# Attention with conditioned heads: the kept exponentials of every fourth step in place of second scores

## The chip, the cores and the metric

The kernel runs on one core of one Trainium2 chip. The metric is the device time of one execution in microseconds (us). One execution of the kernel before was also recorded by the hardware profiler; the page, the busy times by stretch, the chain of waits and the timelines of the engines that are shown below all come from that one execution.

## The reference

Eight batches of 512 rows with 512 features go through one attention layer with 16 heads of 32 features, and the result is added to the input. The conditioning vector of a batch is projected by the same weights and added to the queries and the keys.

```python
Q = split_heads(x @ Wq.T + bq);  K = split_heads(x @ Wk.T + bk);  V = split_heads(x @ Wv.T + bv)
cQ = Q + split_heads(tokens @ Wq.T + bq)
cK = K + split_heads(tokens @ Wk.T + bk)
scores = einsum('bhqd,bhkd->bhqk', cQ, cK) / sqrt(32)
attn = softmax(scores, axis=-1)
out = einsum('bhqk,bhkd->bhqd', attn, V)
return x + merge_heads(out)          # x: (8, 512, 512), all float32
```

## The kernel before

**Steps.** The work is cut into T = 32 steps. Step t is batch t // 4 and a group of four heads (t % 4); the four heads lie in the four groups of 32 partitions. The scores of a step are computed twice. The *row scores* (`row_scores`, L526) have a query row in each partition, 128 query rows at a time (`qc`, four of them): VectorE takes each row's maximum (`one_max` L494, `row_max_of` L535), and ACT takes the exponentials of the row with the maximum as bias (`denominators`, L545), of which only their sum is used: the 512 exponentials go to a tile named "dead". The *second scores* (`exponentials`) have a key in each partition, 128 keys at a time (`kc`): a matmul of ones with the transposed maxima `maxT` subtracts the maximum (L597), the product of keys and queries is accumulated on it (L600), and ACT writes the exponentials to tiles "e" (L611). These have the layout that the product with the values needs (`times_v`, L616).

**The maxima** reach `maxT` in this way: POOL splits each into three bf16 parts (`split_max`, L559 to L562), and a transposing DMA on SP's queue turns them (`turn_max`, L571). The second scores of the next step begin with it.

**The loop** runs over t from 0 to T - 4 (L833). A step has four items. Each does the second scores of step t for one `kc`, the row scores of step t + 1 (the last item: of step t + 2) for one `qc`, and then one more piece of work on TensorE:

- first item: part of the projection q of the next batch; second item: the values of step t - 1 (`weighted`, L616; this item is called V below); third item: part of k; fourth: part of v.
- A projection is done for two head groups at a time by a scheme of seven block products (`product`, L407): `first_products` in one step (VectorE: a copy m1 at L442, then adds at L451, L452, L429 or L432), `other_products` in the following one (adds at L465, L466, L429 or L432). The sums of input blocks that the scheme needs, `xc`, are made by `combine_x` on VectorE.
- VectorE also turns the input blocks (`turn_x`, L323) and the results (`send`, L672) in 32x32 blocks; POOL scales the result and adds the residual (L673, L674), which `load_residual` has loaded and to which POOL has added a bias (L173).

The last three steps (T - 3 to T - 1) have code of their own.

**Order.** The order on PE, ACT, VectorE and POOL is the order in which the program writes the instructions. SP issues nearly all the DMAs from one queue, in an order that the framework's scheduler sets; a DMA there that waits holds up those behind it.

**PSUM.** All eight banks are one ring tile. Which bank plays which part (four for the second scores, four for the row scores, two of these again for the item's own product) is a written table, `TURNS`, of one row per item.

Of the kernel before, what the change touches and what calls it, by code (L numbers as in the profile page):

```python
# [9 lines left out]
F32 = mybir.dt.float32  # L10
BF16 = mybir.dt.bfloat16
# [6 lines left out]
def kernel(  # L18
# [51 lines left out]

    const = ctx.enter_context(tc.tile_pool(name="const", bufs=1))
    stage = ctx.enter_context(tc.tile_pool(name="stage", bufs=3))
    xp = ctx.enter_context(tc.tile_pool(name="xp", bufs=4))
    xtp = ctx.enter_context(tc.tile_pool(name="xtp", bufs=2))
    qkp = ctx.enter_context(tc.tile_pool(name="qkp", bufs=3))
    ep = ctx.enter_context(tc.tile_pool(name="ep", bufs=13))
# [33 lines left out]
    turn = [0]  # L110

    def banks(i, n=1):

        j = TURNS[turn[0]][i]
        if n == 1:
            return psum[:, j, :]
        k = TURNS[turn[0]][i + 1]
        return psum[:, j : k + 1 : k - j, :]

    def advance():  # L120
        turn[0] = {7: 0, len(TURNS) - 1: 4}.get(turn[0], turn[0] + 1)
# [10 lines left out]
    def load_x(n, queue=nc.sync):  # L132

        if n < B * NS:
            xs[n] = xp.tile([P, D], F32, tag="x", name=f"x_{n}")
            queue.dma_start(xs[n], x[n // NS, n % NS * P : (n % NS + 1) * P, :])
# [16 lines left out]
    xr = {}  # L153

# [4 lines left out]
    def load_residual(t):  # L159

        b, g = divmod(t, G)
        if turned_by_vector(t):
            xr[t] = op.tile([P, NB, BL], F32, tag="xr", name=f"xr_{t}", bufs=3)
            for h in range(HG):
                nc.sync.dma_start(
                    xr[t][h * BL : (h + 1) * BL], spread(x[b], g * P + h * BL)
                )
            bias = bvs[:, g, :].unsqueeze(1).broadcast_to([P, NB, BL])
        else:

            xr[t] = xT[b][:, g, :]
            bias = bvl.broadcast_to([P, S])
        nc.gpsimd.tensor_tensor(xr[t], xr[t], bias, ALU.add)  # L173

    ws = {}
# [23 lines left out]
    wk0 = op.tile([P, D], F32, tag="dead", name="wk0")  # L199
    nc.scalar.dma_start(wk0, Wk[:P, :])  # L200

    cond_sb = const.tile([B + 2, D], F32, tag="cond", name="cond_sb")
# [33 lines left out]
    split = []  # L236
    for i in range(2):
        m = const.tile([P, NS, HG, HD], BF16, tag=f"split{i}", name=f"split{i}")
        nc.vector.memset(m, 0.0)
        split.append(m)  # L240
# [62 lines left out]
    def transpose_x(n, pt, leaves=nc.vector.tensor_copy):  # L303

        b, sc = divmod(n, NS)
        if b >= B:
            return
        if sc == 0:
            xT[b] = xtp.tile([P, NC, S], F32, tag="xT", name=f"xT_{b}")
        for cc in range(NC):  # L310
            nc.tensor.transpose(  # L311
                pt[:, cc * P : (cc + 1) * P], xs[n][:, cc * P : (cc + 1) * P], ident
            )
        leaves(xT[b][:, :, sc * P : (sc + 1) * P], pt.rearrange("p (c s) -> p c s", c=NC))
        load_block(n + NC)

    def turn_x(n):
        b, cc = divmod(n, NC)
        if b >= B:
            return  # L320
        if cc == 0:
            xT[b] = xtp.tile([P, NC, S], F32, tag="xT", name=f"xT_{b}")
        nc.vector.transpose(xT[b][:, cc, :], xs[n].rearrange("p f i -> p (f i)"))  # L323
        load_block(n + NC)
# [129 lines left out]

    def other_products(n, b, u, dens, small, at):

        dens()
        one_, two_ = banks(at[0]), banks(at[1])
        product(n, b, u, 4, one_[:, :HS])
        product(n, b, u, 5, one_[:, HS:])  # L460
        small()
        product(n, b, u, 2, two_[:, :HS], (1,))
        product(n, b, u, 3, two_[:, HS:])
        c1, c12, c2, c22 = parts_of(n, b, u)
        nc.vector.tensor_tensor(c12, one_[:, HS:], c12, ALU.add)  # L465
        nc.vector.tensor_tensor(c2, halves(one_), twice(c22), ALU.add)  # L466
        plus(n, b, u, 0, c1, halves(two_), c1)
        if n != "v":
            for g in range(2):
                qkT[n, b * G + u * 2 + g] = pair_of(b * G + u * 2, n)[:, g, :]  # L470
# [27 lines left out]
    def row_max(t, qc, hold=False):  # L498

        if t >= T:  # L500
            return
        open_max(t)
        for j in range(HG):
            row_scores(t, qc, j, banks(HG + j))
        if t < T - 2 or t * NS + qc == T * NS - 1:
            for j in range(2):
                one_max(t, qc, j, banks(HG + j))
        else:
            row_max_of(t, qc, 0, banks(HG, 2))
        last, both = [banks(HG + 2), banks(HG + 3)], banks(HG + 2, 2)  # L510

        def held():
            if hold and t < T - 2:
                for j in range(2):
                    one_max(t, qc, 2 + j, last[j])
            else:
                row_max_of(t, qc, 1, both)

        if hold:
            return held  # L520
        held()
        return nothing
# [16 lines left out]
    def denominators(t, qc, prs=range(NP)):  # L539

        if t >= T - 2:
            return
        for j in [pr * 2 + i for pr in prs for i in range(2)]:
            dead = op.tile([P, S], F32, tag="dead", name=f"dead_{t}_{qc}_{j}")
            nc.scalar.activation(  # L545
                dead,
                banks(HG + j),
                AF.Exp,
                bias=nmax[t][:, qc, j, :],
                accum_out=sums[t][:, qc, j, :],  # L550
            )

    def split_max(t, on=nc.gpsimd):

        if t >= T:
            return
# [9 lines left out]
    def turn_max(t):  # L566

        if t >= T:
            return
# [22 lines left out]
    def exponentials(t, kc, at=None):  # L592

        bank = [psum[:, i, :] for i in at] if at else [banks(i) for i in range(HG)]
# [18 lines left out]
    def times_v(t, kc, pt, chunks=range(NS)):  # L613
        b, g = divmod(t, G)
        for j in range(HG):
            nc.tensor.matmul(  # L616
                pt[j * HD : (j + 1) * HD, :],
                vs[b % 2][:, kc, (g * HG + j) * HD : (g * HG + j + 1) * HD],
                es[t, kc, j // 2][:, j % 2, :],
# [13 lines left out]

    def masked(t):

        apart = op.tile([P, HG, NS, NS], F32, tag="apart", name=f"apart_{t}")
# [17 lines left out]

    def weighted(t, pt, pd, between):
# [8 lines left out]
        rec = op.tile([P, NB, 1], F32, tag="recs", name=f"recs_{t}")  # L664
        nc.vector.reciprocal(rec, pd[:, :NB].unsqueeze(2))
# [24 lines left out]
    def condition(n, pt):  # L690
# [4 lines left out]
        part[n] = const.tile([P, D], F32, tag=f"part{n}", name=f"part_{n}")  # L695
# [21 lines left out]
    def bank(i):  # L717
        return psum[:, i, :]
# [86 lines left out]

    def part_of(t, pt, of, between=None):
# [5 lines left out]
        if t in parts:  # L812
            p = op.tile([P, S], F32, tag="dead", name=f"part_{t}_{of[0]}")
# [19 lines left out]
    for t in range(T - 3):  # L833
        b, r = divmod(t, G)

        exponentials(t, 0)
        held = row_max(t + 1, 1, r % 2)
        of = ((t - 1) // G + 1, (t - 1) % G)
        dens = lambda: denominators(t + 1, 1)
        if t:  # L840
            project_pair("q", *of, dens, nothing, 1 if r % 2 else (0, 3), held)
        else:
            first_products("v", 0, 0, dens, nothing, 1)
            turn_x(NC + 2)
            load_residual(1)
        turn_x(t + NC + 3)
        advance()

        exponentials(t, 1)
        row_max(t + 1, 2)  # L850
        dens = lambda: denominators(t + 1, 2)
        if t:
            dens()
            weighted(
                t - 1, banks(0), banks(1), lambda: combine_x(b + 1, r) if r < 2 else None
            )
        else:
            dens()
            other_products("v", 0, 0, nothing, nothing, (0, 2))
        advance()  # L860

        exponentials(t, 2)
        rest = row_max(t + 1, 3, r % 2)

        def held():
            rest()
            split_max(t + 1)
            turn_max(t + 1)

        dens = lambda: denominators(t + 1, 3)  # L870
        if t:
            project_pair("k", *of, dens, nothing, 1 if r % 2 else (0, 3), held)
        else:
            held()
            first_products("v", 0, 1, dens, nothing, 1)
            combine_x(1, 0)
        if t:
            load_residual(t + 1)
        advance()

        exponentials(t, 3)
        held = row_max(t + 2, 0, r % 2)
        dens = lambda: denominators(t + 2, 0)
        project_pair("v", *of, dens, nothing, 1 if r % 2 else (0, 2), held)
        advance()

# [55 lines left out]

    t = T - 3
# [7 lines left out]
    load_residual(t + 1)  # L951
    load_residual(t + 2)
# [15 lines left out]
    apart = masked(t - 1)  # L968
    part_of(t - 1, banks(2), [2, 3])
# [35 lines left out]
    den = op.tile([P, NB, BL], F32, tag="dead", name=f"den_{t - 1}")  # L1005
# [23 lines left out]
    part_x = op.tile([P, S], F32, tag="dead", name="part_x")  # L1029
    nc.vector.tensor_tensor(part_x, pd, xr[t], ALU.mult)  # L1030
    den = op.tile([P, S], F32, tag="dead", name="den")
    nc.scalar.copy(den, pd)
    store_30(nc.scalar, (2,))
    oT = op.tile([P, S], F32, tag="res_last", name="oT", bufs=1)
    y = op.tile([P, NS, P], F32, tag="xr_last", name="res", bufs=1)
# [58 lines left out]
```

## Time and profile before

| | |
|---|---|
| median of 3 runs | 716.9 us (715.38 to 716.99) |
| profiled execution, whole time | 717.11 us |
| its span, from first to last instruction | 715.0 us |
| mean granted TensorE clock | 0.998 |
| busy: PE, ACT, VectorE (DVE), POOL | 705.7, 604.7, 535.3, 176.5 us |
| DMA | 33.43 MB, mean 47 GB/s |

Busy time is time in which an engine executes something; matmuls are pipelined, so a busy PE is not PE at its peak. PEld is the loading of weights beside the matmuls. A group of instructions is named by its line in the code, its engine, what it writes and what it reads. A matmul in float32 appears as two records, so "x8" in a timeline of PE is four matmuls. Idle time in brackets stands ahead of an instruction, with the instruction or DMA that ended it.

### The profile page before, as it was taken

What the parts mean: (1) busy time and instruction counts of PE and PEld (TensorE: products, weight loads), DVE (VectorE), ACT (ScalarE), POOL (GpSimd) and SP (SyncE); (2) the same over time, 40 slices, a digit from 0 to 9 for tenths busy, and PEclk for the clock granted to TensorE, in tenths of its full rate; (3) what the DMA queues carried; (4) which work ended last, traced back from release to release, by engine and by line L of the source; (5) the groups of instructions that cost most, each with busy time, mean ns of one, the idle gap of its engine ahead of it and who ended that gap; (6) DMA issues with size and microseconds to landing.
All of it is one profiled execution on the core that took longest, in us unless ns stands there. A gap on an engine that the chain in (4) does not pass through costs nothing.

```text
span 715.0 us, 22748 instructions
## 1 busy us (share of the span) xinstructions
PE 705.7 (99%) x9160; PEld 321.1 (45%) x9160; DVE 535.3 (75%) x918; ACT 604.7 (85%) x1497; POOL 176.5 (25%) x275
## 2 busy tenths in 40 slices
PE   8999999999999999999999999999999999999996
PEld 7445444444444444444444444444444444444431
DVE  4798767877768877778777877777777777667776
ACT  2589888888889899898888889899898898889674
POOL 3712221122221122221122221122221122221451
PEclk9999999999999999999999999999999999999999
DMA  7634321323322323321323321322211222311111
GB/s 181 106 61 68 54 40 29 53 42 51 53 33 41 51 42 50 54 42 32 50 42 52 53 40 32 51 43 49 39 28 17 35 39 39 39 30 19 31 31 30
DMA packets 223390, 33.43 MB, mean 47 GB/s; under 512 B 221610, under 2 KB 222122, under 8 KB 223284
## 3 DMA queue, kind: packets, MB, share of 16 engines
q1 hardware_dynamic: 221524, 30.92, 26.4%
q8 instruction: 72, 1.18, 0.7%
q10 hardware_dynamic: 1760, 1.05, 0.5%
q14 instruction: 34, 0.28, 0.1%
HBM read 19.75 MB, written 8.39 MB: 39 GB/s over the span
## 4 chain that ended last, share of the span: by engine, by line
PE 93%; DVE 2%; DMA 2%; issue 1%; ACT 1%; POOL 0%; SPq 0%; DVEq 0%; POOLq 0%
PE psum L407 39%; PE psum L526 16%; PE psum L616 15%; PE psum L600 14%; PE psum L597 5%; PE psum L350 2%; DMA maxT<-split 1%; DVE acc L894 1%; PE psum L920 1%; DMA w_q<-in_L_cond_Wq_dram 1%; PE psum L266 0%; DVE nmax L535 0%; DVE acc L892 0%; PE psum L694 0%; PE psum L311 0%
## 5 line engine op out<-in xcount | busy, mean ns | idle before, releaser
L545 ACT ACTIVATE dead<-psum,nmax 128x512 f32<-128x512 f32 x480 | 327.4, 706 | 5.6 <-DVE nmax L494 3.1
L611 ACT ACTIVATE e<-psum 128x512 f32<-128x512 f32 x488 | 252.0, 603 | 69.5 <-PE psum L600 69.3
L494 DVE TENSOR_REDUCE nmax<-psum 128x1 f32<-128x512 f32 x324 | 208.3, 685 | 133.4 <-PE psum L526 133.4
L526 PE MATMUL psum<-kT,qT 32*128 32x512 f32 x1024 | 141.1, 598 | 0.0
L673 POOL TENSOR_TENSOR res<-res,recs 128x512 f32<-128x512 f32 x30 | 31.4, 1047 | 419.9 <-DVE res L672 419.9
L600 PE MATMUL psum<-qT,kT 32*128 32x512 f32 x976 | 125.5, 587 | 0.0
L616 PE MATMUL psum<-e,v 128*32 128x512 f32 x1024 | 121.2, 596 | 0.0
L535 DVE TENSOR_REDUCE nmax<-psum 128x2 f32<-128x1024 f32 x88 | 106.8, 1215 | 2.7 <-PE psum L526 2.7
L545 ACT ACTIVATION_READ_ACCUMULATOR dead<-psum,nmax 128x1 f32 x480 | 107.8, 225 | 0.0
L526 PEld LDWEIGHTS psum<-kT,qT 32*128 32x128 f32 x1024 | 59.5, 182 | 55.9 <-ACT dead L545 16.9
L616 PEld LDWEIGHTS psum<-e,v 128*32 128x32 f32 x1024 | 26.6, 110 | 65.1 <-issue 37.6
L407 PE MATMUL psum<-wc_v,xc 128*32 128x256 f32 x768 | 50.2, 379 | 0.0
L600 PEld LDWEIGHTS psum<-qT,kT 32*128 32x128 f32 x976 | 48.6, 185 | 2.2
L597 PE MATMUL psum<-maxT,onesb 3*128 3x512 bf16 x488 | 48.1, 385 | 1.2 <-DMA maxT<-split 1.1
L407 PE MATMUL psum<-xc,wc_k 128*32 128x256 f32 x720 | 47.1, 379 | 0.0
L407 PE MATMUL psum<-xc,wc_q 128*32 128x256 f32 x720 | 47.1, 379 | 0.0
L173 POOL TENSOR_TENSOR xr<-xr,bvs 128x512 f32<-128x512 f32 x31 | 39.4, 1270 | 20.5 <-DMA x<-in_x_dram 13.1
L597 PEld LDWEIGHTS <-onesb 3*128 3x128 bf16 x488 | 12.3, 91 | 65.7 <-issue 60.2
L674 POOL TENSOR_TENSOR res<-res,xr 128x512 f32<-128x512 f32 x30 | 38.6, 1286 | 2.3
L407 PE MATMUL psum<-wT_v,xT 128*32 128x256 f32 x512 | 36.8, 382 | 0.0
L407 PE MATMUL psum<-xT,wT_k 128*32 128x256 f32 x480 | 34.5, 382 | 0.0
L407 PE MATMUL psum<-xT,wT_q 128*32 128x256 f32 x480 | 34.5, 382 | 0.0
(168 smaller groups left out, 710.0 us busy)
## 6 DMA issues: line engine op xcount, KB each, us to landing
xr<-in_x_dram SPq DMA_DIRECT2D x124, 64.0 KB, 2.4
out_dram<-res SPq DMA_DIRECT2D x122, 64.0 KB, 1.9
x<-in_x_dram SPq DMA_DIRECT2D x112, 64.0 KB, 2.4
w_q<-in_L_cond_Wq_dram SPq DMA_DIRECT2D x4, 256.0 KB, 4.2
w_v<-in_L_cond_Wv_dram SPq DMA_DIRECT2D x16, 64.0 KB, 2.3
w_k<-in_L_cond_Wk_dram SPq DMA_DIRECT2D x16, 48.0 KB, 2.4
x<-in_x_dram ACTq DMA_DIRECT2D x2, 256.0 KB, 4.2
x<-in_x_dram SPq DMA_DIRECT2D x2, 256.0 KB, 4.2
```

The costliest lines, as they stand in the source:

```text
L173: nc.gpsimd.tensor_tensor(xr[t], xr[t], bias, ALU.add)
L407: nc.tensor.matmul(pt[r], still[:, r], moving, start=(kc == kcs[0]), stop=(kc == kcs[-1]))
L494: nc.vector.tensor_reduce(nmax[t][:, qc, j : j + 1, 0], pt, AX.X, ALU.max, negate=True)
L526: nc.tensor.matmul(pt, qkT["q", t][r, qc * P : (qc + 1) * P], qkT["k", t][r, :], start=True, stop=True,)
L535: nc.vector.tensor_reduce(nmax[t][:, qc, pr * 2 : pr * 2 + 2, 0], pt, AX.X, ALU.max, negate=True)
L545: nc.scalar.activation(dead, banks(HG + j), AF.Exp, bias=nmax[t][:, qc, j, :], accum_out=sums[t][:, qc, j, :],)
L597: nc.tensor.matmul(bank[j], onesb[r, :], maxT[t][r, :], start=True, stop=False)
L600: nc.tensor.matmul(bank[j], qkT["k", t][r, kc * P : (kc + 1) * P], qkT["q", t][r, :], start=False, stop=True,)
L611: nc.scalar.activation(e[:, i, :], bank[pr * 2 + i], AF.Exp)
L616: nc.tensor.matmul(pt[j * HD : (j + 1) * HD, :], vs[b % 2][:, kc, (g * HG + j) * HD : (g * HG + j + 1) * HD], es[t, kc, j // 2][:, j % 2, ...
L673: nc.gpsimd.tensor_tensor(y, y, rec.broadcast_to([P, NB, BL]), ALU.mult)
L674: nc.gpsimd.tensor_tensor(y, y, xr.pop(t), ALU.add)
```

## The change

Seven steps, t = 3, 7, 11, 15, 19, 23 and 27, become *blocked* steps. For these:

- `denominators` writes the exponentials of the row scores into a tile `blocked[t]` (128 x 8192 floats) in place of "dead", with the four 32-column blocks of each 128 keys sorted apart by an access pattern.
- VectorE turns this tile in place in 32x32 blocks, eight transposes of 128 x 1024 per blocked step (`turn_blocks`): five in the step before (two in its item V, ahead of and behind the result's transpose, and one at the end of each other item), three in the step itself.
- DMAs on SP's queue exchange the block g of partition group a with the block a of partition group g, for the six pairs (a, g) (`swap_blocks`). Each half of the tile takes three moves of six DMAs (32 partitions x 4 KB each): into a spare tile from pool `ep`, across, and back. The moves are placed by the table `SWAPS`: first half after items 3 and 4 of the step before and item 1 of the blocked step, second half after its item 4 and items 1 and 2 of the step behind.
- `times_v` reads `blocked[t]` in place of "e". `exponentials`, `split_max` and `turn_max` are left out for these steps.

Around it, for all steps:

- `denominators` writes the exponentials of the other steps back into the PSUM bank they are read from.
- The item V is the first of its step; in the step behind a blocked step it is the last.
- In blocked steps the q and k products leave PSUM by ACT copies and POOL adds (`first_by_others`).
- `combine_x` runs on POOL in the loop; `turn_x` is done twice in each of two steps out of four, and not in the others; `masked` is made in the third item of its own step.
- The PSUM banks of the loop come from an order that is kept as the loop goes (`begin`, `released`) in place of the table; in a blocked step the row scores use the first four places.
- Pools shrink to make room for one tile of 128 x 8192 floats at a time (`room`): `xp` from 4 to 3, `ep` from 13 to 10, the residual's from 3 to 2, one split buffer for two. The start's and the tail's temporary tiles lie in tiles from `room` too.

```diff
+    BLOCKED = [t for t in range(3, T - 4, G)]
...
+    def turn_blocks(t, units):
+        for n in units:
+            pr = slice(n % NP * 2, n % NP * 2 + 2)
+            e = blocked[t][:, :, n // NP, pr, :].rearrange("p g h s -> p g (h s)")
+            nc.vector.transpose(e, e)
+
+    APART = [(a, g) for a in range(HG) for g in range(a + 1, HG)]
+
+    def swap_blocks(t, half, move):
+        def part(a, g):
+            e = blocked[t][a * BL : (a + 1) * BL, g, half * 2 : half * 2 + 2]
+            return e.rearrange("p c h s -> p (c h s)")
+        if move == 0:
+            between[t, half] = [
+                ep.tile([P, 2, S], F32, tag="e", name=f"between_{t}_{half}_{i}") for i in range(2)
+            ]
+        for n, (a, g) in enumerate(APART):
+            at = (n + 2) % HG * BL
+            kept = between[t, half][n // HG][at : at + BL].rearrange("p i s -> p (i s)")
+            to, of = [(kept, part(a, g)), (part(a, g), part(g, a)), (part(g, a), kept)][move]
+            nc.sync.dma_start(to, of)
...
-            dead = op.tile([P, S], F32, tag="dead", name=f"dead_{t}_{qc}_{j}")
+            if t in BLOCKED:
+                to = blocked[t][:, :, qc, j, :].rearrange("p g (c e) -> p g c e", e=BL)
+            else:
+                to = banks(w + j)
+            of = banks(w + j)
+            if t in BLOCKED:
+                of = of.rearrange("p (c g e) -> p g c e", g=HG, e=BL)
             nc.scalar.activation(
-                dead,
-                banks(HG + j),
+                to,
+                of,
                 AF.Exp,
                 bias=nmax[t][:, qc, j, :],
                 accum_out=sums[t][:, qc, j, :],
...
     def times_v(t, kc, pt, chunks=range(NS)):
         for j in range(HG):
+            if t in BLOCKED:
+                e = blocked[t][:, :, :, j, kc * BL : (kc + 1) * BL].rearrange("p a c e -> p c a e")
+            else:
+                e = es[t, kc, j // 2][:, j % 2, :]
...
+    def first_by_others(n, b, u, dens, small, at):
+        dens()
+        product(n, b, u, 1, one_[:, :HS]); product(n, b, u, 6, two_[:, HS:])
+        product(n, b, u, 2, two_[:, :HS], (0,)); product(n, b, u, 7, one_[:, HS:])
+        nc.scalar.copy(m1, one_[:, :HS])
+        nc.scalar.copy(c1, halves(two_))
+        nc.scalar.activation(c22, one_[:, HS:], AF.Identity, bias=add)
+        for o in (c1[:, 0, :], c12):
+            nc.gpsimd.tensor_tensor(o, o, m1, ALU.add)
+        nc.gpsimd.tensor_tensor(c22, c22, c12, ALU.add)
...
+    TURNED = [((1, 1), (0, 1), (0, 1), (0, 1)), ((0, 0), (0, 1), (0, 1), (0, 1))]
+    SWAPS = {
+        (-1, 2): (0, 0), (-1, 3): (0, 1), (0, 0): (0, 2),
+        (0, 3): (1, 0), (1, 0): (1, 1), (1, 1): (1, 2),
+    }
+    for t in range(1, T - 3):
+        blocks = t in BLOCKED
+        w = 0 if blocks else HG
+        items = ["q", "k", "v", "V"] if t - 1 in BLOCKED else ["V", "q", "k", "v"]
+        for i, item in enumerate(items):
+            rows = (t + 1, i + 1) if i < 3 else (t + 2, 0)
+            begin(w)
+            if not blocks:
+                exponentials(t, i)
+            hold = row_max(*rows, late_first, w)
+            ...
```

## The prediction

> **What bounds the kernel now.** I read the head of the page first, then the busy time by stretches of four steps, to see whether one engine is full all through the loop.
>
> ```profile
> PE 705.7 (99%) x9160; PEld 321.1 (45%) x9160; DVE 535.3 (75%) x918; ACT 604.7 (85%) x1497; POOL 176.5 (25%) x275
> 216.70:302.50 85.80, 85.80 (x1164) 38.53 (x1160) 65.27 (x113) 76.95 (x195) 19.10 (x32) 1.00 0.29 45
> 302.50:388.00 85.50, 84.82 (x1147) 38.17 (x1148) 64.27 (x112) 75.90 (x191) 19.10 (x32) 1.00 0.27 45
> ```
>
> In the second and third line the columns are stretch, length, then busy time of PE, PEld, DVE, ACT and POOL, the granted clock and the DMA share. PE is busy in 85.80 of 85.80 us, at full clock. A busy PE need not be a fast one, so next the chain of waits, over step 12: does it stay on PE, and with what?
>
> ```profile
> 302.52 0.33 PE psum L597 x4
> 302.85 0.86 PE psum L600 x8
> 303.71 0.86 PE psum L526 x8
> 304.57 3.16 PE psum L407 x56
> 307.73 0.33 PE psum L597 x4
> ...
> 341.57 4.32 DMA maxT<-split
> ```
>
> It does. A step has four items; the first begins at 302.52 and the second at 307.73. An item is 0.33 us for the maxima's matmuls (L597), 0.86 us for the second scores (L600), 0.86 us for the row scores (L526), then 3.16 us of projection or, in the item that I call V, the values (L616, 3.6 us). The items last 5.21, 5.70, 5.21 and 5.33 us, a step 21.45 us. The chain leaves PE for maxT alone: its transfer took 4.32 us there. The waits of PE on it are small:
>
> ```profile
> PEld L597 <- DMA maxT<-split: 5.6, 10, 1.2
> PE psum L597 <- DMA maxT<-split: 1.1, 2, 0.7
> ```
>
> That is 6.7 us in all. So matmuls taken from PE come off the span, until another engine or a transfer takes PE's place.
>
> **What is removed.** The blocked steps are 3, 7, ... 27: seven. The order of PE's instructions in the changed kernel shows no matmul of L597's or L600's kind in them, and as many as before in all others. 7 x 4 items x (0.33 + 0.86) us = 33.3 us. A blocked step then needs 21.45 - 4.76 = 16.7 us of PE. ACT loses 16 exponentials there, and maxT with its transfer is not needed.
>
> **VectorE.** It gains 8 block transposes of 128x1024 for each blocked step u: five in step u-1, three in u. No row shows this size; L756 shows 554 ns at 384 columns and 686 at 512, so 1,024 is some 1.21 us by that slope, as the reduction of 1,024 (1215 ns), and 1.13 us after overlap with its neighbour. Where would they go?
>
> ```profile
> 315.50 1.29 DVE L494 TENSOR_REDUCE nmax<-psum 128x1 f32<-128x512 f32 x2 [1.21 <-PE psum L526]
> 316.71 1.22 DVE L535 TENSOR_REDUCE nmax<-psum 128x2 f32<-128x1024 f32 x1
> 317.84 0.41 DVE L465 TENSOR_TENSOR kT<-psum,kT 128x256 f32<-128x256 f32 x1
> 318.17 0.68 DVE L466 TENSOR_TENSOR kT<-psum,kT 128x512 f32<-128x512 f32 x1
> 318.77 0.75 DVE L432 SCALAR_TENSOR_TENSOR kT<-psum,tok,kT 128x512 f32<-128x512 f32 x1
> 320.86 1.29 DVE L494 TENSOR_REDUCE nmax<-psum 128x1 f32<-128x512 f32 x2 [1.34 <-PE psum L526]
> ```
>
> The brackets are VectorE's idle time for the next row scores: 1.2 to 1.3 us at an item's end, one transpose wide, and the change puts one there, behind the adds that free the projections' banks. Step u-1: maxima 4 x 2.33, adds 3 x 1.6, sending 0.8 makes 14.9, and 5 x 1.13 makes 20.6 us of 21.45. Step u: 9.3 + 0.8 + 1.4 (only v's adds) + 3.4 = 14.9 of 16.7. It fits: nothing, with 0 to 1 us per block as bounds if a transpose is a fifth longer. The turning of x and xc's sums leave these steps.
>
> **ACT and POOL.** In the blocked step ACT has 16 denominators, 16 x 0.66 = 10.6 us, and the copies of q and k, each 256 + 512 + 256 columns (L445: 372 to 407 ns at 256, L814: 585 at 512), 2 x 1.3: 13.2 of 16.7. Elsewhere its work stays, but it writes PSUM where it wrote "dead". ACT idles (85.8 - 76.95) / 64 = 0.14 us per denominator, so up to that a slower write is hidden. No row shows ACT writing PSUM; I take the present 706 ns. (The Trainium skill, ScalarE: Activation LUTs, in "Step-by-step: what each stage is for", calls a PSUM destination the faster one for ScalarE; no run here shows it, and it would make the term a gain.) POOL adds the products (three of 256 columns, some 0.65 us each, half of the 1269 ns of L815) and xc's four sums (1.27 us each, on POOL in the rows L333 to L337 at the start), from 4.8 to about 7 us per step: hidden, unless they stand before the split of the maxima. After the q products they end at about 11.8 us of step u, and the maxima that the split needs end at 11.75.
>
> **The exchange.** Each blocked step issues 36 transfers of 128 KB on SP's queue, in two halves of three dependent moves of six. Seven times 4.7 MB is 33 MB, as much as the whole kernel moves now, at a DMA share of 0.28: enough room. Latency is what counts. The first half has step u and most of u+1, some 30 us. The second is tight; in us from the start of step u+1:
>
> - the last transpose ends at 1.6 (step u: v's row scores at 13.4, maxima, m1, adds and transpose 4.9 behind them = 18.3, less 16.7);
> - SP issues a transfer of few long rows in about 0.38 (w_q's median), so move 0 leaves from 1.6 to 3.9, and its first lands at 2.0 + d;
> - two transfers of move 1, then eight x loads stand in SP's order. They wait for VectorE's turning of x (6.65 and 7.3) and cost 0.48 each: until 10.5;
> - four of move 1 until 12.0; the last of move 2 leaves at 12.4 + d and lands at 12.4 + 2d;
> - V, now last in step u+1, begins on PE at 5.21 + 5.21 + 5.33 + 2.05 = 17.8.
>
> PE waits 2d - 5.4 us. The rows that bound d:
>
> ```profile
> w_q<-in_L_cond_Wq_dram SPq DMA_DIRECT2D x4, 256.0 KB, 4.2
> x<-in_x_dram SPq DMA_DIRECT2D x112, 64.0 KB, 2.4
> ```
>
> At 2.4 the wait is 0, at 4.2 it is 3.0. 128 KB lies between; I take the middle, d = 3.3: 1.2 us. Blocks 23 and 27 have no x loads and end 3.8 us sooner: no wait. 5 x 1.2 = 6.0 us (0 to 15). That six are under way at once need not change d: the row nearest to it is the start, where the DMA moved 309 GB/s from 4 to 8 us, and six of 128 KB at that rate take 2.5 us, about SP's issue pace of 6 x 0.38. Queued behind the waiting transfers on SP is maxT of u+2; its split is done at about 15.9 and move 2 issued at 15.7, so it is not late.
>
> A rule of the Trainium skill speaks against this form of exchange: SBUF — State Buffer, "Door 1: The DMA port swizzle", says that 32 partitions reach 8 of the 16 ports (about 218 GB/s), and "The DMA setup-cost knee" adds some 2 us per transfer and advises one transfer over 128 partitions. By its figures one lands in 2.6 us (an estimate), and the wait would be 0; six at once would take 2.0 + 3.6, and at d = 5.6 the wait would be 5.8. The sum above stays with the rows.
>
> **maxT's other places.** After step u: split at 12.9, landing 2.4 to 4.4 later (the spread of maxT's landings), so 15.3 to 17.3 against the next item at 16.7: 0 to 0.6. After step u+2: V of u and u+1 are sent one after the other, each POOL 2.25 and SP 4 x 0.52, xr and x loads between, so SP reaches maxT at 18.2 and it lands at 20.6 to 22.6 against 21.45: 0 to 1.2. Now it is 6.7 us over 12 waits; I add 0.5 per block, 3.5 us (0 to 10).
>
> **Sum.** The profiled execution took 717.1 us, 2.1 of them around its span of 715.0, and the median is 716.9. 717.1 - 33.3 + 6.0 + 3.5 = 693.3, less 0.2 to the median: 693. All waits at their lower ends give 684; all at their upper ends, with 1 us per block on VectorE, leave 33.3 - 15 - 10 - 7 = 1 us of gain. They need not come together: five sixths of that 32 us would be 710.
>
> **Rivals.**
> - *Nothing is given back* (0.20): d under 2.7 and maxT in time, 684. For it: VectorE's and ACT's idle time is as wide as the new work. Against: three dependent moves in one step.
> - *The exchange is late* (0.10), the case that ends slower. Gain and loss balance at 33.3 / 7 = 4.8 us per block. By 2d - 5.4 alone that is d = 5.1; with blocks 23 and 27 waiting 3.8 less and maxT's 3.5 in the sum it is 5.4. At d = 6.5 five blocks wait 7.6 us and two 3.8: with maxT 717.1 - 33.3 + 45.6 + 3.5 = 733. For it: six at once, and x loads of 128 B packets between. Against: the slowest row, at twice the size, has 4.2.
> - *ACT becomes the bound* (0.06): writes to the bank being read cost 0.3 us more. Four per item, 0.16 x 4 = 0.64 us beyond its idle time, over some 90 items, 58 us: 751. The point is 0.14 + 23.8 / 360 = 0.21 us more each. Against: the nearest rows, copies from PSUM by ACT, show nothing of the kind.
> - *The values read slowly* (0.04): V of a blocked step reads runs of 32 elements. At half speed 7 x 3.6 = 25 us: 718, no change. At full speed nothing; all moving rows here are contiguous, and the weights' slices with steps cost PE nothing visible.
> - That it leaves the matmuls in is excluded by the order of instructions.
>
> **How the numbers follow.** The forecast has 0.60. About 0.3% is what a measurement here can tell from no change. Faster: forecast, full gain and the mild ends of the others, 0.86; within 0.3%: the slow values and a balance of waits, 0.04; slower: the late exchange and ACT without their mild ends, 0.10. The range of 684 to 710 takes in full gain, d up to 4.2 with most of maxT's spread; outside lie some 0.05 below and 0.15 above.
>
> **What would show it.** Blocked steps of 16.7 us on PE, steps 21.45 between; PE's waits on the blocks (V's weight loads) near 6 us in all, in steps 4, 8, ... 20 only; maxT's near 10 us; transposes of 1.2 us; landings near 3.3. Wrong would be a wait at V over 4 us, row scores or L600's kind waiting on ACT, or V longer than 3.6 us.

## The result: slower by 0.7%, where 3.3% faster was forecast

| | before | changed |
|---|---|---|
| median of 12 runs each | 715.93 us | 721.48 us |
| lowest to highest | 714.38 to 717.44 | 715.40 to 725.15 |
| profiled execution, span | 715.0 us | 718.0 us |
| PE busy | 705.7 us | 685.8 us |
| mean granted clock | 0.998 | 0.987 |

The ratio to the kernel before is 1.0072, interval 1.0046 to 1.0097. The runs of the changed kernel spread over 10 us, those of the kernel before over 3; the shortest run of the changed kernel had a mean granted clock of 0.991, the longest 0.982. Medians here and below are of all runs, while the ratios leave out the runs that took over 1.5% longer than the fastest of the same kernel (one with the tiny loads, two with the 28 small matmuls).

The head of the changed kernel's page answers to the first line shown of before:

```profile
PE 685.8 (96%) x8824; PEld 314.0 (44%) x8824; DVE 563.6 (79%) x878; ACT 563.2 (78%) x1427; POOL 233.2 (32%) x315
```

PE is busy 19.9 us less, not the 27.4 us less that it should be by its matmuls (33.3 - 5.9, below), and it idles 32.2 us in place of 9.3. The chain of waits around the end of step 12, which stands behind the blocked step 11, shows where. Columns as before: start, length, what.

```profile
312.48 0.42 DVE kT L517
312.91 0.30 SPq L170
...
313.25 0.49 SPq L170
...
313.78 0.58 SPq L170
...
314.40 0.49 SPq L170
...
314.93 0.51 SPq L618
315.49 0.59 SPq L618
316.12 1.92 SPq L618
318.08 0.59 SPq L618
```

The chain has left PE for SP's queue (SPq): issue after issue of the x loads (L170) and of the exchange's moves (L618). PE's own timeline has the two parts of the loss (in brackets the idle time ahead):

```profile
319.53 1.03 PE L579 MATMUL psum<-kT,qT 32*128 32x512 f32 x8
324.55 1.93 PE L709 MATMUL psum<-blocks,v 128*32 128x512 f32 x8 [3.99 <-ACT psum L634]
326.23 0.33 PE L744 MATMUL psum<-apart,modulo 128*32 128x16 f32 x8
326.35 4.55 PE L709 MATMUL psum<-blocks,v 128*32 128x512 f32 x24
330.84 0.40 PE L686 MATMUL psum<-maxT,onesb 3*128 3x512 bf16 x4
```

PE idles 3.99 us ahead of V. (The bracket names ACT; but the last transfer of the exchange was issued from 321.9, and landings in this stretch take 2.3 to 3.9 us with a median of 2.6, which is 324.5. The runs below show which of the two V waited for.) Then V takes 6.3 us, where V of step 23's block takes 3.7. The stretches of V in the busy times say why: the ninth column, ahead of the DMA share, is the granted clock.

```profile
324.50:330.90 6.40, 6.35 (x44) 1.75 (x48) 0.26 (x1) 0.00 (x0) 0.00 (x0) 0.57 0.02 3
583.60:587.40 3.80, 3.80 (x48) 1.12 (x48) 2.58 (x4) 3.80 (x10) 0.00 (x0) 1.00 0.15 29
```

Over the seven blocked steps PE idles 3.92, 2.99, 3.99, 3.46, 3.50, 0 and 0 us at V, 17.9 us in all, and V takes 5.31, 5.40, 6.35, 3.70, 5.39, 3.70 and 3.70 us, 7.7 us more than seven times 3.70. Behind steps 23 and 27, where no x loads stand among the moves, no time is lost in this execution.

### The profile page after: what moved, and what is told of

It is laid out like the page before. It is cut to its first block, busy times and chain, and to the rows that moved or that the text cites. A ratio compares the mean times of both kernels' runs of the same rounds, so it can differ in the third digit from the quotient of the medians.

```text
span 718.0 us, 22033 instructions
## 1 busy us (share of the span) xinstructions
PE 685.8 (96%) x8824; PEld 314.0 (44%) x8824; DVE 563.6 (79%) x878; ACT 563.2 (78%) x1427; POOL 233.2 (32%) x315
## 4 chain that ended last, share of the span: by engine, by line
PE 76%; SPq 7%; DMA 6%; POOL 4%; DVE 2%; ACT 2%; issue 2%; DVEq 0%; POOLq 0%; ACTq 0%
PE psum L435 30%; PE psum L709 16%; PE psum L579 13%; PE psum L689 9%; PE psum L686 4%; DMA maxT<-split 3%; SPq L618 2%; PE psum L378 2%; SPq L778 2%; SPq L170 2%; ACT psum L634 1%; DMA blocks<-between 1%; DVE nmax L546 1%; DMA xr<-in_x_dram 1%; POOL res L775 1%
## 5 line engine op out<-in xcount | busy, mean ns | idle before, releaser
L634 ACT ACTIVATE psum<-psum,nmax 128x512 f32<-128x512 f32 x368 | 244.5, 673 | 29.0 <-DVE nmax L546 21.5
L700 ACT ACTIVATE e<-psum 128x512 f32<-128x512 f32 x376 | 194.1, 603 | 91.2 <-PE psum L689 87.7
L546 DVE TENSOR_REDUCE nmax<-psum 128x1 f32<-128x512 f32 x298 | 191.3, 683 | 83.8 <-PE psum L579 81.4
L689 PE MATMUL psum<-qT,kT 32*128 32x512 f32 x752 | 96.7, 587 | 0.0
L709 PE MATMUL psum<-e,v 128*32 128x512 f32 x800 | 95.3, 597 | 0.0
L634 ACT ACTIVATION_READ_ACCUMULATOR psum<-psum,nmax 128x1 f32 x368 | 78.8, 214 | 0.0
L634 ACT ACTIVATE blocks<-psum,nmax 128x512 f32<-128x512 f32 x112 | 76.1, 717 | 0.0
L599 DVE STREAM_TRANSPOSE blocks<-blocks 128x1024 f32<-128x1024 f32 x56 | 68.5, 1223 | 0.0
L709 PE MATMUL psum<-blocks,v 128*32 128x512 f32 x224 | 33.6, 741 | 17.9 <-ACT psum L634 10.9
L773 DVE STREAM_TRANSPOSE res<-psum 128x512 f32<-128x512 f32 x28 | 20.1, 717 | 29.1 <-PE psum L709 26.1
```

The source lines that it names most:

```text
L546: nc.vector.tensor_reduce(nmax[t][:, qc, j : j + 1, 0], pt, AX.X, ALU.max, negate=True)
L599: nc.vector.transpose(e, e)
L634: nc.scalar.activation(to, of, AF.Exp, bias=nmax[t][:, qc, j, :], accum_out=sums[t][:, qc, j, :],)
L689: nc.tensor.matmul(bank[j], qkT["k", t][r, kc * P : (kc + 1) * P], qkT["q", t][r, :], start=False, stop=True,)
L700: nc.scalar.activation(e[:, i, :], bank[pr * 2 + i], AF.Exp)
L709: nc.tensor.matmul(pt[j * HD : (j + 1) * HD, :], vs[b % 2][:, kc, (g * HG + j) * HD : (g * HG + j + 1) * HD], e, start=(kc == chunks[0]), ...
```

## The experiments

The theories, as the expectations name them. *Theory 1*: PE's wait for the exchange at V, set by the order and the pace of SP's queue, and the clock that falls behind the wait, ate the gain. *Theory 2*: the traffic of the exchange delays every other transfer. *Theory 3*: the rest of the change (order of items, banks, writes to PSUM, sums on POOL) costs what the blocks bring. All ratios are to the kernel before, run on the same chip.

**No blocked step**

```diff
-    BLOCKED = [t for t in range(3, T - 4, G)]
+    BLOCKED = []
```

> The changed kernel with no blocked step: second scores everywhere, no transposes, no exchange; all the rest of the change stays (V first in its step, banks from an order, exponentials of the row scores written to PSUM, xc's sums on POOL, pools and the start's tiles). Theory 1 (PE's wait for the exchange, set by SP's queue, ate the gain) and theory 2 (the transfers' traffic delays every other transfer and ate it): the rest is neutral, 714 to 719 us. Theory 3 (the rest of the change costs what the blocks bring): 735 us or more, since 33 us of matmuls are back.

714.29 us, ratio 0.998 (0.9964 to 0.9996). Theory 3 falls for all that the change does outside blocked steps: that is neutral or a trace faster. What it does in blocked steps alone, the ACT copies and POOL adds of the q and k products, is not in this run.

**The x loads behind the exchange**

```diff
-                    turn_x(t + NC + 2)
-                    turn_x(t + NC + 3)
+                    turn_x(t + NC + 2, False)       # turns, does not load
+                    turn_x(t + NC + 3, False)
...
+            if i == 3 and r == 0:
+                load_block(t + NC + 5)
+                load_block(t + NC + 6)
```

> The eight x loads that stand among the second half's moves on SP's queue are issued at the end of that step instead; the transfers, their sizes and number are the same. Theory 1: the chain of issues is shorter by 8 x 0.55 = 4.4 us, so PE's waits of 3.0 to 4.0 us at V in steps 4, 8, 12, 16 and 20 shrink to below 0.7, TensorE keeps its clock there, and the time falls by 17.9 - 3 + 7.7 = 23 us, to about 698 (694 to 703). Theory 2: the traffic is unchanged, the waits at most halve: 709 to 719. Theory 3: no change beyond 3 us.

696.2 us, ratio 0.9722 (0.9691 to 0.9752): the place of eight loads per block, in five blocks, is worth 3.5% of this kernel (1.0072 - 0.9722). SP's timeline of the same stretch (start, length of the issues together) has the three moves back to back and the x loads behind them:

```profile
295.88 4.02 SPq L619 DMA_DIRECT2D between<-blocks  x6
300.00 3.72 SPq L619 DMA_DIRECT2D blocks<-blocks  x6
303.76 5.15 SPq L619 DMA_DIRECT2D blocks<-between  x6
308.96 1.17 SPq L170 DMA_DIRECT2D x<-in_x_dram  x2
```

PE's idle time ahead of V is gone but for 0.47 us in one place. V of the blocked steps is back at its full pace, and PE is busy 678.2 us.

**No exchange**

```diff
-            nc.sync.dma_start(to, of)
+            pass
```

> All 252 transfers of the exchange are left out (V of the blocked steps then reads blocks that were turned but not exchanged). Theory 1 and theory 2: 721.5 less 25.6 us of wait and slow clock, less what of maxT's waits SP's load causes (0 to 5): 691 to 697. Theory 3: above 705, since the transfers are not what costs.

696.22 us, ratio 0.9731 (0.9704 to 0.9757). Leaving all 252 transfers out brings no more than moving eight others out of their way: in the version with the x loads moved, the exchange costs nothing that can be measured. PE still waits 8.5 us for maxT here (1.1 us in the kernel before), so most of that wait does not come from the exchange.

**V from a resident tile**

```diff
-                e = blocked[t][:, :, :, j, kc * BL : (kc + 1) * BL].rearrange("p a c e -> p c a e")
+                e = wT["v"][:, kc, :]
```

> The exchange runs in full, but V of the blocked steps multiplies a resident weight tile instead of the exchanged exponentials, so that nothing on PE waits for the exchange. Theory 1: as without the exchange, up to 4 us more: 692 to 700. Theory 2: the traffic still delays maxT, x and the residuals, so most of the loss stays: 708 or more.

699.35 us, ratio 0.9767 (0.9731 to 0.9804). The transfers with their traffic are all there, only nobody on PE waits for them. Theory 2 falls; the few microseconds above the two runs before are mostly waits of PE for maxT (12.1 us in all against 6.6 with the x loads moved, 1.83 at the longest), which still stands behind the moves in the queue. ACT's work is the same here and V no longer waits, so it was the exchange that V waited for, not ACT as the bracket had it.

**Tiny loads in the x loads' place.** To the version with the x loads moved:

```diff
...
+                        for h in range(HG if n < B * NC else 0):
+                            nc.sync.dma_start(
+                                xs[n][h * BL : (h + 1) * BL, 0, :], x[0, :BL, :BL]
+                            )
```

> As the kernel with the x loads moved to the step's end (696.2 us), with eight tiny loads (32 rows of 128 B, 4 KB each, whose data nothing reads) in the place on SP's queue where the x loads stood. Theory 1a (each issue occupies SP for about half a microsecond, whatever it moves): the chain is 3 to 4 us longer again, PE waits 2 to 3.5 us at V in five steps and most of the clock's loss returns: 708 to 720. Theory 1b (the x loads' 512 packets each in the rings ahead of the moves): tiny loads cost nothing, 694 to 699.

725.05 us, ratio 1.0072 (1.0044 to 1.0101): with a sixteenth of the bytes there, the whole loss is back, and more than the 720 us expected. V waits 2.16 to 3.92 us in six places, not five: the tiny loads stand behind step 23 too, where no x loads stood, and V waits 3.12 us there in place of 0. SP's timeline of step 12:

```profile
304.93 4.99 SPq L619 DMA_DIRECT2D between<-blocks  x6
310.01 1.18 SPq L619 DMA_DIRECT2D blocks<-blocks  x2
311.24 3.93 SPq L1037 DMA_DIRECT2D x<-in_x_dram  x8
315.21 2.91 SPq L619 DMA_DIRECT2D blocks<-blocks  x4
318.17 3.77 SPq L619 DMA_DIRECT2D blocks<-between  x6
```

Eight tiny loads take 3.93 us to issue here, and 3.82 to 4.79 over the six places; the eight full ones took 4.45 here, and 4.45 to 5.63 over their five. Most of the cost is an instruction's turn in SP's queue, whatever it moves (1a, not 1b); a sixteenth of the bytes takes some 0.1 us off each.

**Small matmuls ahead of V**

```diff
+        if t in BLOCKED[:5]:
+            for _ in range(28):
+                nc.tensor.matmul(pt[:, :P], onesb, onesb, start=True, stop=True)
```

> The changed kernel as it was, with 28 small matmuls of ones (2.95 us in the start of the kernel before) ahead of V's first matmul in steps 4, 8, 12, 16 and 20, so that TensorE idles for less than 1.1 us there; V can begin no sooner. If the clock drops because of the idle time, V takes 3.7 us there again and the time falls by up to the 7.7 us that V took longer: 711 to 717. If V was slow for another reason (runs of 32 elements, freshly written data), the time stays at 719 to 724.

724.09 us, ratio 1.0067 (1.0036 to 1.0097): no change. It settles nothing: the 28 ran back to back in 1.74 us, in place of the 2.95 that I had read off the start, so 1.46 to 2.74 us of idle time were left, and V was slow again in four of the five places. With 60:

> The changed kernel with 60 small matmuls of ones ahead of V in steps 4, 8, 12, 16 and 20; 28 of them took 1.74 us there and left 1.5 to 2.7 us of idle time, so 60 take some 3.7 us and leave less than 0.5. V waits for the exchange as before. If idle time drops the clock, V runs in 3.7 us in all seven places with the granted clock at 1.00, and the time against the kernel before falls from 1.007 to about 0.997 (0.992 to 1.001). If something else slows V, it still takes 5.3 us or more there and the ratio stays at 1.005 to 1.009.

716.21 us, ratio 1.0004 (0.9982 to 1.0026), by ratios 0.7% or some 4.9 us better than the changed kernel, near the upper end of what was expected. V now takes its full pace in four of the five places, behind idle times of 0.32 to 1.18 us. The fifth had 1.95 us, and shows what idle time does (timeline of PE in step 16; the granted clock over this V was 0.68):

```profile
403.59 3.52 PE L764 MATMUL psum<-onesb 128*128 128x128 bf16 x60
409.06 1.07 PE L709 MATMUL psum<-blocks,v 128*32 128x512 f32 x8 [1.95 <-DMA blocks<-between]
410.01 4.45 PE L709 MATMUL psum<-blocks,v 128*32 128x512 f32 x24
```

In these places V still could not begin before the exchange had landed; only its pace changed. The small matmuls write the bank that V writes and ran at once, so that bank was free. So the slow V came from the idle time, not from the 32-element runs that it reads.

**Two blocked steps**

```diff
-    BLOCKED = [t for t in range(3, T - 4, G)]
+    BLOCKED = [23, 27]
```

> Only steps 23 and 27 are blocked, the two behind which no x loads stand in SP's queue. Each saves 4.76 us of matmuls, pays 4 x 0.21 us at its row scores' start and some 0.5 us of waits for maxT: 3.4 us each, 6.8 in all from the 714.3 us (0.998) of no blocked step: ratio 0.987 to 0.991. If a blocked step costs PE anything else that the x loads only made worse, the ratio stays above 0.994.

708.49 us, ratio 0.9889 (0.9867 to 0.9911), as expected. Against 0.998 with none, each of these two blocks brings 0.46%, 3.3 us. One of them was not wholly unhindered in the profiled execution: behind step 23 the six issues of the last move took 5.56 us, in place of 3.8, and V waited 1.15 us.

**The kernel before without the maxima's matmuls.** *Row-tiled* are here the matmuls whose rows carry the form `32*128` (second scores and row scores; the maxima's have `3*128`), *column-tiled* those with `128*32` (projections and V).

```diff
-            nc.tensor.matmul(bank[j], onesb[r, :], maxT[t][r, :], start=True, stop=False)
```

> The kernel before without the matmuls of ones with maxT (L597), so that the exponentials come out without the maximum taken off. The changed kernel's row scores took 1.07 us in blocked steps, against 0.86 behind second scores. If the first row-tiled group behind column-tiled ones always pays these 0.21 us, L597's 0.33 us hid it, and taking it away saves only 122 x 0.12 = 15 us: 699 to 705. If the 0.33 us are all its own, it saves 40 us: 674 to 680.

708.46 us, ratio 0.9871 (0.9856 to 0.9885): 9.3 us for 122 groups, 0.08 us each, less than the 0.12 of the first case, and the time lies above its 699 to 705. In its chain of waits the group that comes first behind the column-tiled products is now the second scores (L597 in this run), and takes longer:

```profile
299.62 1.07 PE psum L597 x8
300.69 0.86 PE psum L526 x8
```

The second scores take 1.07 us in every item shown of that stretch, where they took 0.86 behind the maxima. By that the 40.3 us of the maxima's matmuls (122 x 0.33) come down to 14.7. The row scores behind them take 0.86 us in some items and up to 1.09 in others, and their matmuls are busy 147.7 us in place of 141.1; that is where the other 5 us lie, and why is not settled.

**All that stood in the way moved.** The x loads of both steps that turn x, the residual's load and bias of the step behind a blocked one, and the q products' adds on POOL (now behind the split of the maxima):

```diff
...
+            if i == 3 and r == 0:
+                load_block(t + NC + 5)
+                load_block(t + NC + 6)
+            if i == 0 and r == 2:
+                load_block(t + NC + 5)
+                load_block(t + NC + 6)
+            if i == 3 and r == 1 and t > 1:
+                load_residual(t)
+            if i == 3 and (r != 0 or t == T - 4):
...
+                    while pending:
+                        pending.pop()()             # the q products' adds on POOL
```

> The changed kernel with all that stood ahead of maxT or of the exchange moved behind it: x loads at the end of the step behind a blocked step and at the start of the step before one, the residual's load and bias of the step behind a blocked one moved one step on, and POOL's adds of the q products behind the split of the maxima. Theory 1: V's waits go as in the run with the x loads moved (696.2), and of maxT's waits there (PE idle of some 8 us) more than half goes too: 688 to 693. Theory 2: no better than 696.

688.94 us (688.70 to 690.11), ratio 0.9601 (0.9586 to 0.9615). This version beats both kernels. The waits for maxT, of weight loads (PEld) and of matmuls (PE), first in the changed kernel, then in this version:

```profile
PEld L686 <- DMA maxT<-split: 12.1, 11, 2.2
PE psum L686 <- DMA maxT<-split: 7.1, 7, 1.8
PEld L696 <- DMA maxT<-split: 3.9, 5, 1.1
PE psum L696 <- DMA maxT<-split: 1.6, 3, 0.6
```

Added as in the prediction that is 5.5 us, against 6.7 before and 19.2 in the changed kernel; of PE's own idle time it is 1.6 us, against 1.1 and 7.1. Which of the moved pieces takes the most off is not separated. The page of this version shows what bounds it:

```profile
PE 678.0 (99%) x8824; PEld 312.8 (46%) x8824; DVE 562.9 (82%) x878; ACT 563.3 (82%) x1427; POOL 232.5 (34%) x315
```

PE idles 687.4 - 678.0 = 9.4 us of its span, as before (9.3).

## Why the prediction was wrong

**The step that failed** is the term of the exchange, "PE waits 2d - 5.4 us", 6.0 us in all, where 17.9 were measured; in it, the price of an issue: "SP issues a transfer of few long rows in about 0.38 (w_q's median)". The trace of after has 0.59 for the moves, and single ones of up to 2.0:

```profile
L618 SPq DMA_DIRECT2D between<-blocks x84: 512/590/1896, 106.2 to 652.6; - x84
L618 SPq DMA_DIRECT2D blocks<-blocks x84: 512/588/1917, 110.8 to 657.4; - x84
L618 SPq DMA_DIRECT2D blocks<-between x84: 513/589/2000, 114.6 to 661.2; - x84
```

(Columns: shortest, median and longest issue in ns.) Followed through the chain in step 12, which begins at 302.8, in us from there:

| | predicted | measured |
|---|---|---|
| move 0 begins to be issued | 1.6 | 2.1 |
| move 0 all issued | 3.9 | 6.3 |
| x loads all issued | 10.5 | 12.1 |
| move 1 all issued | 12.0 | 15.9 |
| move 2 all issued | 15.7 | 19.7 |
| V can begin | 19.0 | 21.7 |
| V could begin for PE's sake | 17.8 | 17.8 |

The places were right: V's wait is in steps 4, 8, 12, 16 and 20 and in no others, and the x loads make it. But I let the landing time d govern it, let it stand in the chain twice, and gave it the whole uncertainty. d was measured at 2.3 to 2.6 us, below my 3.3; with 2.6 the formula gives no wait at all, where 3.99 us were measured. In the trace the first issue of move 2 follows the last of move 1 by 0.05 us, so d stands in the chain once, behind the last move, and issues fill the rest: 26 of them take 17.6 us (2.1 to 19.7), where my prices give 18 x 0.38 + 8 x 0.48 = 10.7. The kernel before had the nearer row in its own SP timeline (x loads at 0.48 each); half a microsecond was the safer reading, and still somewhat low. The bound "0 to 15" for this term was built on d alone.

**What was not in the sum.** The wait of 3.6 us on average came with a second price: in four of the five places the granted clock of TensorE fell to 0.57 to 0.69 over V, which cost 7.7 us more. Of the signs that the prediction named, this one showed: V longer than 3.6 us. The trace of before has no PE idle time in the loop beyond 0.7 us and so could not show it. A page would have warned: the Trainium skill, TensorE: Matmul & The Clock Gate, "Why this matters for your kernels", asks for no idle gaps above about 3 us. Here gaps of 2.99 to 3.99 us were followed by the slow clock in four cases of five (not the one of 3.46 us). So were shorter ones, such as 1.95 us behind the 60 small matmuls and 2.60 us in the run with the tiny loads; by these runs the page's limit is too high.

**Also missing**: 5.9 us. In blocked steps the row scores are the first row-tiled matmuls behind column-tiled ones, and take 1.07 us from start to start, 0.21 more than the 0.86 that I read behind the second scores: 28 x 0.21. The chain of after shows it in step 11:

```profile
290.18 1.07 PE psum L579 x8
```

The run without the maxima's matmuls has the same 1.07 us for other matmuls at that place. What makes it, the change of form or the load of the first weights, is not separated.

The wait at V alone would not have left the range: without the 7.7 and the 5.9 us, which the prediction put at nothing, the median would be 721.5 - 13.6 = 707.9, within 684 to 710.

**The new sum**, in spans of the profiled executions: -33.3 of matmuls + 5.9 at the row scores + 7.7 of slow clock + 17.9 of V's waits + 5.0 of other idle time (the matmuls' waits for maxT alone rose by 6.0) = +3.2, measured +3.0.

**What held.** The saving of 33.3 us on PE: in the run with the x loads moved, busy time falls from 705.7 to 678.2, which is 33.3 - 5.9 within 0.1. VectorE: the 56 block transposes took 1.223 us each (1.21 forecast) and fit the idle time, as the last version shows, in which they all stand and PE idles no more than before. ACT: 673 ns for a denominator written to PSUM against 706 to SBUF, so the rival in which ACT becomes the bound had the wrong sign, as the rule of the Trainium skill that the prediction cites (ScalarE: Activation LUTs, "Step-by-step: what each stage is for") would have it. The values' runs of 32 elements are read at full pace (593 ns median, 592 before). maxT's term (3.5 us, 0 to 10) was too small but within its bounds: 6.0 us of PE's own idle time. The 6.7 us of before, from which it was built, add weight loads' waits, part of which run beside PE's work; PE's own were 1.1, and by the added figure the sign "near 10 us" was missed with 19.2. And what the prediction named as its condition for POOL came about: in the chain of after, from 385.15 us on, POOL's adds of the q products (L504, L505) stand ahead of the split and of maxT's transfer.

**The rivals.** The kernel ended slower, as the late exchange has it, but only in part by that rival's account. The exchange was late by the pace of issues and not by d, and the waits came to 17.9 us at V and 5.0 elsewhere, short of the 33.3 at which gain and loss balance. It took the 7.7 us of clock and the 5.9 us at the row scores, which no rival had, to turn the gain into a loss; that the outcome is this rival's is partly luck. At 0.10 I had it too low all the same: with three dependent moves of six on one in-order queue and others' loads between them, 0.2 us more for each of the 18 moves' issues is 3.6 us of the 4.8 per block at which it begins.

## What to carry to other kernels

Before a transfer chain is put on a queue that also serves others, count every issue that stands between its first and its last transfer, whoever it belongs to, and price each by the slowest like it in the trace; latency hides in parallel, issues do not. Give the chain its place first and move whatever has time behind it. An engine that is to be relieved must not be made to wait instead: a wait on TensorE was paid here nearly one and a half times, once as idle time and once as clock.

## What the runs showed of the hardware

- Eight issues in a row on SP's queue took 3.82 to 4.79 us for loads of 4 KB in 32 rows and 4.45 to 5.63 us for loads of 64 KB in 512 rows, so 0.5 to 0.7 us each; a move of 128 KB between SBUF and SBUF took 0.59 us (median).
- The clock fell behind most idle times of 2 to 4 us, and V of 3.70 us then took 5.3 to 6.35 in the changed kernel. Over the traces of the changed kernel, of the tiny loads and of the small matmuls (28 and 60), V was slow behind 14 of the 16 idle times of 1.95 to 3.99 us, not behind those of 2.16 and 3.46, and behind none of up to 1.46. The limit is not sharp in these runs, and where it lies stays open.
- The first group of row-tiled matmuls behind column-tiled ones took 1.07 us, 0.21 more than behind other row-tiled ones. A small group at that place is nearly free: the maxima's matmuls, 0.33 us in the chain, are worth 0.08.
